# Adding rows and output biases in DRAM by an accumulating transfer instead of on GpSimd, and giving the root its constant as a bias

## The chip, the cores and the metric

The kernel runs on one core of one Trainium2 chip. The metric is device time in microseconds (us) of one execution, and lower is better. In this text PE is TensorE, PEld its weight loads, DVE is VectorE, ACT is ScalarE, POOL is GpSimd, and SP is SyncE, which here only issues transfers. "Sequence" means one of the four batch entries, counted from 0.

## The reference

The input x has 4 sequences of 2048 tokens with 512 features, all in fp32. With xn the layer norm of x, the output is x + attention(xn) + ffn(xn).

```python
xn = (x - mean) / sqrt(var + 1e-5)                  # over the 512 features
qkv = xn @ qkv_w.T + qkv_b                          # 16 heads of 32
attn = softmax(q @ k.T * 32 ** -0.5)
att = (attn @ v) @ proj_w.T + proj_b
idx = top_k(xn[:, 0, :] @ Wr + br, 2)               # two of 8 experts per sequence
ffn = sum over the two of (gelu(xn @ W1[e] + b1[e]) @ W2[e] + b2[e]) / 2
out = x + att + ffn
```

What the change is about are two small pieces of this. The first is the term that each output row starts from: x + proj_b + (b2[e0] + b2[e1]) / 2. The second is the square root in the layer norm.

## The kernel before, in words

The work of a sequence is cut into *units*. A unit takes 4 heads (a group), 512 queries (a chunk `qc`) and 128 keys (`kt`). There are 16 units to a chunk, 4 chunks to a group, 4 groups to a sequence, 1024 units in all, and 22 units of lead before unit 0. One loop over `U` writes out by hand, for each engine, what belongs to a unit: the scores `s` with their shift (L725, L733), a first pass for the maxima `m` that runs 22 units ahead (L715, reduced by DVE in L855), the exponentials `p` on ACT (L849), and the weighting by v (`acc`, L745). POOL adds up the exponentials of a chunk (`add_weights`): it starts with L762 at `kt` 1, goes on with L766, and at `kt` 15 it issues a transfer that accumulates the last `p` into `psum` (L764). There are four `p` buffers, so the exponentials of a unit need the buffer that was used four units earlier.

The class `Plan` puts all the rest into slots at every second unit: products for the next q and k, v projections, the two expert layers (`w1`, `w2`), the output projection (`proj`), and, for the next sequence, statistics, root, normalisation and the block sums (`ws`, `tx`) on POOL. It also gives each load a unit at which SP issues it; SP issues everything in one queue, in the order in which the loop reaches it. All PSUM tiles come from one pool of 8 banks, taken in turn.

The places that the change touches:

- `load`, tag `row` (L373): for the first of the two experts (`k` = 0) a row tile of 128 tokens is loaded from x, for the second one from `part_dram`, where the first left its partial sum. In `w2`, DVE adds half of the expert's product to it (L633).
- `row_ready`: four units after a `k` = 0 row has been loaded, POOL adds the sequence's `bias` tile to it (L881). The `bias` tile is made once per sequence by `load_bias` and `sum_bias` (L662 to L664).
- `root` (L431): DVE adds EPS to the variances (L433), ACT takes the root (L434), DVE the reciprocal (L435), POOL makes the shift (L436, L437). It is called once for the 4 first tokens, four times at the start for sequence 0, and once each for sequences 1 to 3, one unit into group 2 of the sequence before.
- The lead: the 16 tiles of v of sequence 0 are projected one per unit (`project_v`, L514). The tile has two buffers (`vrow`), and each is stored to `v_dram` by SP two units later (L515). Calls put into `later(u, ...)` are made at the end of unit `u`.

Of the kernel before, what the change touches and what calls it, by code (L numbers as in the profile page):

```python
# [9 lines left out]
F32 = mybir.dt.float32  # L10
BF16 = mybir.dt.bfloat16
U32 = mybir.dt.uint32
AF = mybir.ActivationFunctionType
ALU = mybir.AluOpType
# [3 lines left out]
P = 128  # L18
# [4 lines left out]
EPS = 1e-5  # L23
CH = 512
# [13 lines left out]
class Plan:  # L38
# [6 lines left out]
    def __init__(self, B, DC, NCH, NT, TPC):  # L45
# [13 lines left out]
        for G in range(1, B * DC):  # L59
            b, g = divmod(G, DC)  # L60
# [16 lines left out]
        for b in range(1, B):  # L77
# [8 lines left out]
            for n in range(NT):  # L86
                self.extra.setdefault(q1 + 2 * (16 + n) + 1, []).append(("stats", b, n))
                c, i = divmod(n, TPC)
# [80 lines left out]
        for s in slots:  # L169
            for it in self.items.get(s, []):  # L170
                if it[0] == "w2":
                    rows_at[it[1], it[3]] = s + 3
                assert it[0] != "proj" or s - 2 * WARN >= rows_at[it[1], it[2]], (s, it)
                for tag, key in self.needs(it):
                    self.uses.append((s, tag, key))
                if it[0] == "w2" and it[4] == 0:
                    self.first_load["row", (it[1], it[3], 1, it[5])] = s + 4
        for s in range(slots[0], self.units):
# [13 lines left out]
        for u in range(2, self.units + 1, 2):  # L192
            kt, G = (u - 2) % NT, (u - 2) // self.per_group
# [45 lines left out]
def block_kernel(  # L239
# [16 lines left out]
    nc = tc.nc  # L256
    B, N, D = x.shape
    E = Wr.shape[1]
    DC = D // P
    NT = N // P  # L260
    NCH = N // CH
    TPC = CH // P
# [3 lines left out]
    LEAD = plan.lead  # L266

    ctx.enter_context(tc.manual_schedule())
    const = ctx.enter_context(tc.tile_pool(name="const", bufs=1))
# [11 lines left out]
        return slice(j * HD, (j + 1) * HD)  # L281


    xn_dram, t_dram, v_dram, att_dram, part_dram, ws_dram = {}, {}, {}, {}, {}, {}
    for b in range(B):
        for k in range(TOP_K):
            ws_dram[b, k] = tc.dram_tile([P, DC, D], F32, name=f"ws_dram_{b}_{k}")
# [1 line left out]
    for b in range(B):  # L289
        for c in range(NCH):  # L290
            xn_dram[b, c] = tc.dram_tile([P, DC, CH], F32, name=f"xn_dram_{b}_{c}")
            v_dram[b, c] = tc.dram_tile([P, TPC, D], F32, name=f"v_dram_{b}_{c}")
            att_dram[b, c] = tc.dram_tile([P, DC, CH], F32, name=f"att_dram_{b}_{c}")
            t_dram[b, c] = tc.dram_tile([P, DC, CH], F32, name=f"t_dram_{b}_{c}")
            for i in range(TPC):
                part_dram[b, c, i] = tc.dram_tile([P, D], F32, name=f"part_dram_{b}_{c}_{i}")
# [6 lines left out]
    def expert(b, k):  # L303
        if (b, k) not in experts:
            experts[b, k] = nc.values_load(
                chosen[b : b + 1, k : k + 1], engines=[SP], min_val=0, max_val=E - 1,
                skip_runtime_bounds_check_because="max_index gives columns of E scores",
            )
        return experts[b, k]
# [3 lines left out]
    def load_xt(t, b, p, i):  # L313

        if i in (1, 2, 3):
            src, h = xn_dram[b, 2 * p + (i == 3)], int(i != 1)
        else:
            src, h = t_dram[b, 2 * p + (i in (7, 6))], int(i in (4, 6))
        nc.sync.dma_start(t, src[:, 2 * h : 2 * h + 2, :])

    def load_wt(t, kind, b, n, i):


        r, h = {1: (0, 0), 2: (0, 1), 4: (1, 1), 6: (0, 0), 3: (0, 1), 7: (1, 0), 5: (1, 1)}[i]
        if kind == "qk":
            if i in (1, 2, 4):
                src = qkv_wT.rearrange("(c p) n -> p c n", p=P)[:, :, (1 - r) * D : (2 - r) * D]
            else:
                src = wqk_dram[r]
            nc.sync.dma_start(t[:, :, 0, :], src[:, 2 * h : 2 * h + 2, ts(n, P)])  # L330
            return
        if i in (1, 2, 4):
            src = W1[ds(expert(b, n), 1)].rearrange("o (c p) f -> p (o c) f", p=P)
        else:
            src = ws_dram[b, n]
        for q in range(2):
            nc.sync.dma_start(t[:, :, q, :], src[:, 2 * h : 2 * h + 2, ts(2 * q + r, P)])

    def x_rows(b, c):
        return x[b, ts(c, CH), :].rearrange("(t p) d -> p t d", p=P)  # L340

    def load(tag, key):
        name = f"{tag}_" + "_".join(str(k) for k in (key if isinstance(key, tuple) else (key,)))
        shape = {"xq": [P, DC, CH], "xt": [P, 2, CH], "xl": [P, TPC, D], "wb": [P, DC, D],
                 "wt": [P, 2, 2, P], "row": [P, D], "prow": [P, D]}.get(tag, [P, TPC, P])
        t = stream.tile(shape, F32, tag=tag, name=name, bufs=BUFS[tag])
        held[tag, key] = t
        if tag == "xq" and key[0] == "stage":
            return t
        if tag == "xq":  # L350
            nc.sync.dma_start(t, xn_dram[key])
        elif tag == "xt":
            load_xt(t, *key)
        elif tag == "wt":
            load_wt(t, *key)
        elif tag == "v":
            b, g, c = key
            nc.sync.dma_start(t, v_dram[b, c][:, :, ts(g, P)])
        elif tag == "xl" and key[0] == "at":
            nc.sync.dma_start(t, att_dram[key[1:]])  # L360
        elif tag == "xl" and key[0] == "w1raw":
            src = W1[ds(expert(*key[1:]), 1)].rearrange("o (c p) f -> p (o c) f", p=P)
            nc.sync.dma_start(t, src)
        elif tag == "xl":
            nc.sync.dma_start(t, x_rows(*key[1:]))
        elif tag == "wb" and key[0] == "proj":
            nc.sync.dma_start(t, proj_wT.rearrange("(c p) n -> p c n", p=P))
        elif tag == "wb" and key[0] == "v":
            nc.sync.dma_start(t, qkv_wT.rearrange("(c p) n -> p c n", p=P)[:, :, 2 * D :])
        elif tag == "wb":  # L370
            src = W2[ds(expert(*key[1:]), 1)].rearrange("o (c p) f -> p (o c) f", p=P)
            nc.sync.dma_start(t, src)
        elif tag == "row":  # L373
            b, c, k, i = key
            src = part_dram[b, c, i] if k else x[b, c * CH + i * P : c * CH + (i + 1) * P, :]
            nc.sync.dma_start(t, src)
        else:
            nc.sync.dma_start(t, part_dram[key])
        return t
# [3 lines left out]
    make_identity(nc, ident)  # L383
    ident_b = const.tile([P, P], BF16, name="ident_b")
    nc.vector.tensor_copy(ident_b, ident)
    ones = const.tile([P, HD], F32, name="ones")
    nc.gpsimd.memset(ones, 1.0)
    ones_b = const.tile([P, P], BF16, name="ones_b")
# [4 lines left out]
    for i in range(2):  # L393
        t = const.tile([P, TPC, GH, HD], BF16, name=f"spread{i}")
# [17 lines left out]
    for n in range(2):  # L412
        wkq.append(stream.tile([P, DC, D], F32, tag="h", name=f"wkq_{n}", bufs=2))
        src = qkv_wT.rearrange("(c p) n -> p c n", p=P)[:, :, (1 - n) * D : (2 - n) * D]
# [5 lines left out]
    for n in range(2):  # L420
        src = qkv_wT.rearrange("(c p) n -> p c n", p=P)[:, :, (1 - n) * D : (2 - n) * D]
# [8 lines left out]

    def root(mv, sd, nb, a, z, np_=P):  # L431

        nc.vector.tensor_scalar(sd[:np_, a:z], mv[:np_, a:z, 1], EPS, None, ALU.add)  # L433
        nc.scalar.activation(sd[:np_, a:z], sd[:np_, a:z], AF.Sqrt)  # L434
        nc.vector.reciprocal(sd[:np_, a:z], sd[:np_, a:z])  # L435
        nc.gpsimd.tensor_tensor(nb[:np_, a:z], mv[:np_, a:z, 0], sd[:np_, a:z], ALU.mult)  # L436
        nc.gpsimd.tensor_scalar(nb[:np_, a:z], nb[:np_, a:z], -1.0, None, ALU.mult)  # L437
# [21 lines left out]
    mv, sd, nb = stat_tiles("first")  # L459
# [31 lines left out]
    hT, bias, b1s = {}, {}, {}  # L491
# [169 lines left out]
    def sum_bias(t, other, pb):  # L661
        nc.gpsimd.tensor_tensor(t, t, other, ALU.add)  # L662
        nc.gpsimd.tensor_scalar(t, t, 0.5, None, ALU.mult)
        nc.gpsimd.tensor_tensor(t, t, pb, ALU.add)  # L664


    mv, sd, nb = stat_tiles(0)

# [34 lines left out]
    def later(u, do):  # L703
        waiting.setdefault(u, []).append(do)
# [119 lines left out]
    for n in range(2):  # L824
        later(3 - LEAD, lambda n=n: nc.sync.dma_start(wqk_dram[n], wkq[n]))
    sum_bias(*load_bias(0))
    row_ready = {}

    for U in range(-LEAD, plan.units):
        second = U >= 0  # L830
        first_pass = U + LEAD if U + LEAD < plan.units else None
        chunk, kt = divmod(U, NT)
        b, g, qc, _ = place(U) if second else (0, 0, 0, 0)
# [42 lines left out]
        if before is not None and kt == (12 if keys == 4 else 14):  # L876
            divide(before)
            later(U + 3, lambda w=before: nc.sync.dma_start(
                att_dram[w[0], w[2]][:, w[1], :], att[w]))
        for t, key in row_ready.pop(U, []):  # L880
            nc.gpsimd.tensor_tensor(t, t, bias[key[0]], ALU.add)  # L881
        if second:
            add_weights(U)

# [10 lines left out]
        for step, sb, n in plan.extra.get(U, []):  # L895
# [10 lines left out]
            else:  # L906
                c, i = divmod(n, TPC)
# [10 lines left out]
        for do in waiting.pop(U, []):  # L918
            do()
        for s, tag, key in loads.get(U, []):  # L920
            t = load(tag, key)
            if tag == "row" and key[2] == 0:
                row_ready.setdefault(U + 4, []).append((t, key))
        if g == 2 and qc == 0 and kt == 0 and second and b + 1 < B:
            new_bias = load_bias(b + 1)
        if g == 2 and qc == 0 and kt == 5 and second and b + 1 < B:
            sum_bias(*new_bias)

        for n, c in ((16, NCH - 1), (1, NCH - 2)):
            if U == plan.units - n:  # L930
                tags = ("xq", "xq") if c == NCH - 1 else ("xl", "h")
                t, rows = (
                    stream.tile([P, TPC, D], F32, tag=tag, name=f"end_{c}_{n}",
                                bufs=BUFS.get(tag, 2))
                    for n, tag in enumerate(tags)
                )
# [7 lines left out]
    U = plan.units  # L944
# [72 lines left out]
```

## Time and profile before

| | |
|---|---|
| time before, median of 3 runs | 5038.61 us (5038.29 to 5046.06) |
| profiled execution, its own time | 5042.55 us |
| profiled execution, its span | 5040.8 us |
| mean granted TensorE clock | 0.997 |
| busy, share of the span | PE 98%, DVE 74%, ACT 47%, POOL 88% |
| POOL, row plus bias (L881) | 64 instructions, 83.8 us |
| POOL, accumulating transfer (L764) | 63 issues, 54.6 us |
| DVE, variance plus EPS (L433) | 8 instructions |

The profile comes from one execution, whose own time stands in the table. Busy shares are averages over the whole span. A busy PE is not PE at its peak. Where the granted clock falls below 1, PE is busy and slow.

### The profile page before, as it was taken

The numbers are of one execution on the slowest core, as the hardware profiler recorded it, in microseconds if no ns is written. First come the engines' busy times: TensorE is split into PE (matmuls) and PEld (weight loads), VectorE is DVE, ScalarE is ACT, GpSimd is POOL, SyncE is SP. The second block draws the span as 40 slices with busy tenths as digits, with TensorE's granted clock in tenths as the row PEclk, the third lists the DMA queues.
The fourth block names the chain that finished last, engine by engine and source line by source line (L and its number), as shares of the span: only waits on it lengthen the run. The fifth ranks groups of instructions, "written<-read, shape, count | busy, mean of one in ns | idle before, by whom it ended". The sixth has DMA issues, their size and how long they took to land. (4 is left out here: it accounts for less than half of the span.)

```text
span 5040.8 us, 107883 instructions
## 1 busy us (share of the span) xinstructions
PE 4947.0 (98%) x45028; PEld 1725.8 (34%) x45028; DVE 3740.2 (74%) x5909; ACT 2394.0 (47%) x4406; POOL 4429.2 (88%) x1498
## 2 busy tenths in 40 slices
PE   8999999999999999999999999999999999999998
PEld 2333333333333333333333333333333333333332
DVE  5777887777777788777777777877777777777762
ACT  1445445454444545454444444555444445454453
POOL 2799998999898998999889998999988988999981
PEclk9999999999999999999999999999999999999999
DMA  6333334433233434434224234434423343323312
GB/s 219 111 103 117 115 96 127 142 122 109 80 107 104 126 107 122 140 114 141 89 86 125 85 121 118 146 122 136 134 70 106 100 123 101 101 80 101 107 62 95
DMA packets 297128, 568.16 MB, mean 113 GB/s; under 512 B 24636, under 2 KB 144188, under 8 KB 279744
## 3 DMA queue, kind: packets, MB, share of 16 engines
q1 hardware_dynamic: 287568, 495.19, 29.4%
q0 software_dynamic: 9072, 66.06, 6.7%
q8 instruction: 354, 5.80, 0.5%
q14 instruction: 134, 1.10, 0.1%
HBM read 367.44 MB, written 127.66 MB: 98 GB/s over the span
## 5 line engine op out<-in xcount | busy, mean ns | idle before, releaser
L766 POOL TENSOR_TENSOR psum<-psum,p 128x2048 f32<-128x2048 f32 x819 | 3722.4, 4545 | 167.6 <-ACT p L849 129.2
L849 ACT ACTIVATE p<-s 128x512 f32<-128x512 f32 x4096 | 2118.0, 603 | 2364.9 <-PE m L715 2181.8
L855 DVE TENSOR_REDUCE mx<-m 128x1 f32<-128x512 f32 x4096 | 2544.2, 684 | 570.1 <-PE m L715 569.8
L733 PE MATMUL s<-qT,kT 32*128 32x512 f32 x8192 | 1919.1, 588 | 0.0
L715 PE MATMUL m<-kT,qT 32*128 32x512 f32 x8192 | 1911.3, 590 | 6.4 <-ACT h L524 3.4
L715 PEld LDWEIGHTS m<-kT,qT 32*128 32x128 f32 x8192 | 920.9, 184 | 334.9 <-issue 244.7
L745 PE MATMUL acc<-p,v 128*32 128x512 f32 x8192 | 988.5, 600 | 37.0 <-ACT p L849 37.0
L733 PEld LDWEIGHTS s<-qT,kT 32*128 32x128 f32 x8192 | 768.6, 185 | 29.2 <-issue 7.3
L485 PE MATMUL ops<-wb_w,h 128*32 128x512 f32 x4096 | 466.0, 595 | 0.6 <-ACT p L849 0.2
L745 PEld LDWEIGHTS acc<-p,v 128*32 128x32 f32 x8192 | 214.2, 109 | 737.0 <-ACT p L849 420.5
L762 POOL TENSOR_TENSOR psum<-p,p 128x2048 f32<-128x2048 f32 x63 | 287.5, 4563 | 203.2 <-ACT p L849 203.2
L754 DVE TENSOR_TENSOR sacc<-acc,sacc 128x512 f32<-128x512 f32 x448 | 309.9, 692 | 158.3 <-PE acc L745 158.3
L485 PE MATMUL hps<-xt,wt_w 128*32 128x512 f32 x3584 | 411.0, 596 | 2.5 <-ACT p L849 2.0
L725 PE MATMUL s<-negm,ones_b 32*128 32x512 bf16 x4096 | 405.7, 385 | 6.2 <-ACT p L849 5.9
L485 PE MATMUL qkps<-xt,wt_qk 128*32 128x512 f32 x3360 | 387.8, 599 | 9.8 <-ACT p L849 9.2
L725 PEld LDWEIGHTS <-ones_b 32*128 32x128 bf16 x4096 | 103.2, 91 | 858.2 <-issue 858.1
L870 DVE RECIPROCAL sums<-sums 128x128 f32<-128x128 f32 x252 | 237.6, 943 | 0.7 <-ACT sums L784 0.7
L485 PEld LDWEIGHTS ops<-wb_w,h 128*32 128x32 f32 x4096 | 120.0, 109 | 308.6 <-issue 229.8
L633 DVE SCALAR_TENSOR_TENSOR row<-ops,row 128x512 f32<-128x512 f32 x128 | 88.4, 691 | 170.3 <-PE ops L485 116.3
L485 PE MATMUL prps<-wb_proj,xl_at 128*32 128x512 f32 x1792 | 203.9, 595 | 0.3
L485 PEld LDWEIGHTS hps<-xt,wt_w 128*32 128x32 f32 x3584 | 103.3, 109 | 268.2 <-issue 186.1
L485 PEld LDWEIGHTS qkps<-xt,wt_qk 128*32 128x32 f32 x3360 | 97.3, 110 | 273.9 <-issue 181.6
(123 smaller groups left out, 1981.6 us busy)
## 6 DMA issues: line engine op xcount, KB each, us to landing
xt<-t_dram SPq DMA_DIRECT2D x181, 512.0 KB, 4.3
xt<-xn_dram SPq DMA_DIRECT2D x133, 512.0 KB, 5.0
psum<-p POOLq DMA_DIRECT2D x63, 1024.0 KB, 8.2
part_dram<-row SPq DMA_DIRECT2D x128, 256.0 KB, 2.0
v_dram<-v SPq DMA_DIRECT2D x64, 256.0 KB, 2.7
wt_w<-ws_dram SPq DMA_DIRECT2D x128, 128.0 KB, 3.3
v<-v_dram SPq DMA_DIRECT2D x64, 256.0 KB, 4.9
row<-in_x_dram SPq DMA_DIRECT2D x64, 256.0 KB, 6.5
```

Source lines behind the costliest of these rows:

```text
L485: nc.tensor.matmul(pp[rows_of(j), :], lhsT[:, rows_of(j)], rhs, start=(first and n == 0), stop=(last and n == len(terms) - 1),)
L633: nc.vector.scalar_tensor_tensor(row, pp, 0.5, row, ALU.mult, ALU.add)
L715: nc.tensor.matmul(t, qT[b, g, qc][r, ts(i, P)], kT[b, g, kc][r, :], start=True, stop=True)
L725: nc.tensor.matmul(tiles[j], ones_b[r, :], negm[b, g, qc][r, :], start=True, stop=False)
L733: nc.tensor.matmul(tiles[j], kT[b, g, kt // TPC][r, ts(kt % TPC, P)], qT[b, g, qc][r, :], start=False, stop=True,)
L745: nc.tensor.matmul(acc[r, :], held["v", (b, g, kt // TPC)][:, (kt + n) % TPC, r], pT[u + n][:, j, :], start=(n == 0), stop=(n == 1),)
L754: nc.vector.tensor_tensor(t, acc, t, ALU.add)
L762: nc.gpsimd.tensor_tensor(psums[b, g, qc], pT[u - 1], pT[u], ALU.add)
L766: nc.gpsimd.tensor_tensor(psums[b, g, qc], psums[b, g, qc], pT[u], ALU.add)
L849: nc.scalar.activation(pT[U][:, j, :], tiles[j], AF.Exp, scale=SCALE)
L855: nc.vector.tensor_reduce(dst, t, AX.X, ALU.max, negate=True)
L870: nc.vector.reciprocal(sums[before][:, q], sums[before][:, q])
```

## The change

There is a new DRAM tensor per chunk, `base_dram`. SP copies the chunk's rows of x into it from DRAM to DRAM (`copy_rows`, 1 MB in 512 rows of 2 KB). Later POOL issues a transfer that accumulates the `bias` tile, repeated four times, into it (`add_bias`, also 512 rows of 2 KB). A `k` = 0 row is then loaded from `base_dram` and is complete when it lands, so L881 and `row_ready` go.

For sequence 0 the four copies are made at unit -18 and the four additions at unit -10. For sequence b + 1 the copies are made at units 6, 8, 10 and 12 of group 2 of sequence b, and the four additions together at unit 16, the first of that group's second chunk. The instructions of PE stand in the same order as before, and SP's other transfers too.

In `root`, DVE's addition of EPS goes; ACT takes EPS as the bias operand of the root and reads the variances itself.

```diff
@@ Plan
+                if it[0] == "w2" and it[4] == 0 and it[1]:
+                    self.first_load["row", (it[1], it[3], 0, it[5])] = (
+                        (it[1] - 1) * self.per_seq + 2 * self.per_group + NT + 1
+                    )
...
+            base_dram[b, c] = tc.dram_tile([P, TPC, D], F32, name=f"base_dram_{b}_{c}")
...
-            src = part_dram[b, c, i] if k else x[b, c * CH + i * P : c * CH + (i + 1) * P, :]
+            src = part_dram[b, c, i] if k else base_dram[b, c][:, i, :]
...
+    eps = const.tile([P, 1], F32, name="eps")
+    nc.gpsimd.memset(eps, EPS)
...
     def root(mv, sd, nb, a, z, np_=P):
-        nc.vector.tensor_scalar(sd[:np_, a:z], mv[:np_, a:z, 1], EPS, None, ALU.add)
-        nc.scalar.activation(sd[:np_, a:z], sd[:np_, a:z], AF.Sqrt)
+        nc.scalar.activation(sd[:np_, a:z], mv[:np_, a:z, 1], AF.Sqrt, bias=eps[:np_])
         nc.vector.reciprocal(sd[:np_, a:z], sd[:np_, a:z])
...
+    def copy_rows(b, c):
+        nc.sync.dma_start(base_dram[b, c], x_rows(b, c))
+
+    def add_bias(b, c):
+        nc.gpsimd.dma_start(
+            base_dram[b, c], bias[b].unsqueeze(1).to_broadcast([P, TPC, D]), accum_op=ALU.add
+        )
...
     sum_bias(*load_bias(0))
-    row_ready = {}
+    for c in range(NCH):
+        later(4 - LEAD, lambda c=c: copy_rows(0, c))
+        later(12 - LEAD, lambda c=c: add_bias(0, c))
...
-        for t, key in row_ready.pop(U, []):
-            nc.gpsimd.tensor_tensor(t, t, bias[key[0]], ALU.add)
...
-            t = load(tag, key)
-            if tag == "row" and key[2] == 0:
-                row_ready.setdefault(U + 4, []).append((t, key))
+            load(tag, key)
...
             sum_bias(*new_bias)
+            for c in range(NCH):
+                later(U + 1 + 2 * c, lambda c=c: copy_rows(b + 1, c))
+        if g == 2 and qc == 1 and kt == 0 and second and b + 1 < B:
+            for c in range(NCH):
+                add_bias(b + 1, c)
```

More of the change, by code (lines that the diff above doesn't have):

```diff
@@ L281, in rows_of @@
         return slice(j * HD, (j + 1) * HD)
-    xn_dram, t_dram, v_dram, att_dram, part_dram, ws_dram = {}, {}, {}, {}, {}, {}
+    base_dram, xn_dram, t_dram, v_dram, att_dram, part_dram, ws_dram = {}, {}, {}, {}, {}, {}, {}
     for b in range(B):
```

## The prediction

> **What bounds the kernel now.** I read the page's busy rows first, then the waits, then the timeline around every place where PE stands still.
>
> ```profile
> PE 4947.0 (98%) x45028; PEld 1725.8 (34%) x45028; DVE 3740.2 (74%) x5909; ACT 2394.0 (47%) x4406; POOL 4429.2 (88%) x1498
> ```
>
> PE is the bound: 94 us of the 5040.8 are free of it, about 17 of them before the lead and 6 in the last products. PE's order stays, so the change is worth only what it takes from or adds to those 94 us, and to the stretches in which PE runs at a lower granted clock. POOL at 88% isn't the bound, and its 83.8 us of row additions are no gain as such. The waits say where POOL and DVE reach PE:
>
> ```profile
> ACT p L849 <- DMA psum<-p: 36.3, 9, 7.4
> ...
> ACT sd L434 <- DVE sd L433: 30.8, 7, 6.5
> ```
>
> (total us, times, longest.) The second is the root. Its timeline in sequence 0, columns start, duration, engine:
>
> ```profile
> 761.40 1.28 ACT L434 ACT_TABLE_LOAD   x1
> 761.74 4.90 DVE L433 TENSOR_SCALAR sd<-mv 128x16 f32<-128x16 f32 x1
> 761.82 4.78 POOL L762 TENSOR_TENSOR psum<-p,p 128x2048 f32<-128x2048 f32 x1
> ...
> 766.67 0.21 ACT L434 ACTIVATE sd<-sd 128x16 f32<-128x16 f32 x1 [3.99 <-DVE sd L433]
> ...
> 767.43 1.21 PE L715 MATMUL m<-kT,qT 32*128 32x512 f32 x1 [3.45 <-ACT h L524]
> ```
>
> The same DVE instruction takes 170 ns at the median of its eight. Here it ends with POOL's pass; in the other two big roots too (4.29 us and 4.28 us). ACT waits behind it, and PE for ACT. Then comes a second price, PE's clock (the last columns are granted clock, DMA share, GB/s):
>
> ```profile
> 767.40:774.00 6.60, 6.57 (x30) 1.77 (x34) 2.89 (x5) 3.34 (x5) 3.50 (x3) 0.53 0.66 185
> ...
> 3207.00:3211.00 4.00, 4.00 (x28) 1.20 (x24) 1.54 (x3) 1.00 (x3) 2.92 (x1) 0.57 0.91 240
> ```
>
> The first wait is POOL's lateness at chunk ends: the accumulating transfer L764 goes out late, and ACT gets its `p` buffer late.
>
> ```profile
> 1160.23 1.07 PE L485 MATMUL qkps<-xt,wt_qk 128*32 128x512 f32 x8 [0.97 <-ACT p L849]
> 2068.41 1.09 ACT L849 ACTIVATE p<-s 128x512 f32<-128x512 f32 x2 [3.25 <-DMA psum<-p]
> 3446.61 0.66 PE L455 MATMUL xt<-ident,xl_normal 128*128 128x128 f32 x4 [2.07 <-ACT p L849]
> 4791.84 1.50 PE L485 MATMUL hps<-xt,wt_w 128*32 128x512 f32 x12 [0.75 <-ACT p L849]
> ```
>
> **What it removes.** *The root.* In sequence 0 ACT would take the root at 762.7, right after its table load, since the variances are there from 753.1. What is left is two table loads and the root, 1.28 + 0.21 + 1.28 = 2.8 us of ACT; a gelu with its tables takes 4.5 us of ACT and costs PE 1.16 us, so this costs PE nothing much. DVE then waits at the reciprocal for ACT until 763.2, some 1.4 us, with the maxima queued behind it. The reciprocal is not held by POOL: L870 never takes more than 953 ns of a 943 ns mean under a POOL that is 88% busy. Gain: 3.45 us plus 6.6 us x (1 - 0.53) = 3.1, 6.5 us. In the third big root (3200) 1.46 plus 4 us x (1 - 0.57) = 1.7, 3.2 us. In the second (1979.7) ACT is in a gelu and a table load until 1983.8 anyway, and the reciprocal holds DVE as long as L433 did: nothing of its 1.48. At the start five small L433 (0.14 to 0.17 us) leave the chain to the first product: 0.3 us.
>
> *64 row additions*, 1.28 us each. They matter in the chunks before a wait: 3 lie before the 0.97, 6 (7.7 us of POOL) before 2068, where PE stood 1.29 us, 6 before the 2.07, and 3 before the 0.75. ACT's waits there are 2.9 to 4.0 us or less, below what is freed, so all four go: 5.1 us. The larger ones (4.73 us at 2368, 2.47 at 3049, 4.97 at 4939) have no row addition in their chunk and stay. DVE's waits for L881 (9.8 us) end no wait of PE.
>
> Together 15 us; I count 14, as the root keeps something.
>
> **What it adds.** *Four copies in the lead, 4 MB on SP's queue.* They stand behind the store of v tile 1 and ahead of that of tile 2.
>
> ```profile
> 68.03 0.81 SPq L825 DMA_DIRECT2D wqk_dram<-wkq  x2
> 68.93 4.28 SPq L515 DMA_DIRECT2D v_dram<-v  x2
> ...
> 77.48 0.32 SPq L581 DMA_DIRECT2D ws_dram<-xl_w1raw  x1
> ```
>
> ```profile
> 77.40 0.69 DVE L514 TENSOR_TENSOR v<-vps,bv_bc 128x512 f32<-128x512 f32 x1 [1.73 <-DMA v_dram<-v]
> ...
> 81.46 0.69 DVE L514 TENSOR_TENSOR v<-vps,bv_bc 128x512 f32<-128x512 f32 x1 [0.97 <-PE vps L485]
> ```
>
> The reader is to see that tile 3 (77.40) waited for tile 1's store, which took 8.4 us for 256 KB as two 1 MB stores were ahead of it. In the same way tile 4 (81.46) will wait for tile 2's store, and so for four copies. Their price is not in the trace. The nearest row, the 1 MB `wqk` stores, landed 2.95 us apart (71.93 and 74.88). The Trainium skill speaks against it: "DMA: Bandwidth & Descriptors", section "Latency and other measured facts", gives copies between HBM tensors 207 to 214 GB/s, which makes an estimate of 4.9 us per MB. Tile 1's data is through at about 75.3. Tile 2 lands 2.4 us after the copies: at 89.5 by the row, at 97.3 by the rule. PE doesn't stand at once: a unit takes 4.64 us and 5 of 8 banks, so with tile 4's bank held it can still do a unit and two maxima, to about 86.9. It goes on 0.8 us after the landing. PE's stop is 3.4 us by the row, 11.2 by the rule, and a stop of 3.45 us has cost 3.1 us of clock. I take 4.2 us per MB, between, nearer the rule since the row moves data on one HBM side only: 8.4 + 3.1 = 11.5 us (ends 3.4 and 14.3). Behind SP's blocked queue stand the store of `ws_dram`, the next `xl_w1raw` load and POOL's block sums, some 10 to 15 us late; the products that need them come 30 us later.
>
> *Four additions in the lead.* POOL idles from 102 to 131.85, so their issue is free. But SP's transfers keep the engines 0.92 busy from 110 to 128, and v stores must land within two units; one already held DVE 1.7 us at 128.4. An accumulated MB lands after 8.2 us (`psum<-p`), so four are up to 33 us of shared engines. Bounds 0 and 10 us; I take 2.5, because DVE's delay has to pass the same 5 us of banks.
>
> *Copies in the loop*, 12 of them, two units (10 us) apart, each under 5 us. The tightest load behind one is the second normalisation load of each sequence: it landed at 822.2 for 829.4, at 2034.2 for 2038.8. The copy ahead is through before SP reaches it. Zero; without that cover about 1 to 5 us each.
>
> *Additions in the loop*, four together on POOL, three times, at the start of a chunk, where POOL waits anyway:
>
> ```profile
> 839.04 0.90 POOL L764 DMA_DIRECT2D psum<-p  x1 [0.30 <-POOL psum L766]
> 847.62 4.56 POOL L762 TENSOR_TENSOR psum<-p,p 128x2048 f32<-128x2048 f32 x1 [7.69 <-ACT p L849]
> ```
>
> L764 takes 0.87 us with 128 rows of 8 KB; an addition has 512 rows of 2 KB. In proportion that is 3.5 us; by the skill (the same page, "Anatomy of one DMA — SWDGE (gpsimd) path") generating descriptors is small and many go out before it shows, so 0.9. Four make 3.5 to 14 us. I take 2 us each, 8: it fits the 7.69 above, at 2061 it takes the place of six row additions, and at 3277 POOL has 4.89 + 1.71 us of idle time. I count 1 us for all, with 22 us of transfer beside loads that have 8.9 us to spare or more.
>
> **Sum:** -14 + 11.5 + 2.5 + 1 = +1 us, on the profiled execution's 5042.55 (span 5040.8 and 1.75 around it). That execution is 3.9 us above the median of 5038.61, so the forecast is 5040 us. About 0.2%, 10 us, is what a measurement of this kernel can tell from no change.
>
> **Rivals.**
> - *Faster.* Copies run at the row's 2.95 us or better, and PE's stop stays below 3.4 us and keeps the clock: -14 + 2 to 4 = 5028. For it: both directions of transfer show about 3 us per MB alone. Against: a copy loads HBM twice. Chance 0.22.
> - *Slower, by POOL.* An addition costs by its rows, 3.5 us. Then 14 us in the chunk meet 11.6 us of idle time at 840 to 865 (7.69 + 2.97 + 0.90), none at 2061, where POOL is 6.5 us late instead of on time, and 10 us at 3277. The lateness shows at the next chunk end as ACT's wait for `psum<-p`: 2.4 + 5.7 + 4 us for PE and up to 3 us of clock each, 12 to 21 us: 5052 to 5061. It decides from about 2.5 us an issue. For it: 512 rows instead of 128. Against: the rule. Chance 0.18.
> - *Slower, in the lead.* Copies of 6 us per MB (PE stops 15.6 us, 18.7 with the clock) and 6 us for the additions: -14 + 25, 5050. Chance 0.14.
> - *That rows from DRAM come too late:* the first is loaded at 153.9, when the additions have long been issued, and used 32 us later. I give it no chance of its own.
>
> **Numbers.** Same 0.46, faster 0.22, slower 0.18 + 0.14 = 0.32. The likeliest case alone spans 5030 to 5048. For 8 in 10 the range goes from 5026, the faster case with all gains, to 5061, POOL's case.
>
> **What would show it.** The root's ACT wait of 3.99 gone and PE without a gap near 764. One DVE wait of 7 to 16 us for `v_dram<-v` near 81, a gap of PE after 87, and a low clock behind it. Copies landing 4 to 5 us apart. The four waits at chunk ends gone, those at 2368, 3049 and 4939 still there. The POOL issue of an addition near 2 us. I am wrong if tile 2's store lands before 86, or if POOL is later than before at the ends of the chunks with additions.

## The result, and the profile after

The changed kernel takes 5057.18 us in the median of 7 runs (5053.79 to 5058.61), against 5039.66 us for the kernel before (7 runs, 5036.28 to 5047.1). The ratio is 1.0029, with a 95% interval of 1.0018 to 1.004: slower by some 15 us (17.5 by the medians). The profiled execution took 5054.43 us, span 5052.7. A profile line has the line numbers of its own kernel: in the changed kernel L514 of the kernel shown has become L520, L715 L730, L764 L779 and L849 L866; the copy is L673 and the addition L677. In the experiments they lie a few lines off.

Busy times, from the page of the changed kernel:

```profile
PE 4952.9 (98%) x45028; PEld 1730.8 (34%) x45028; DVE 3726.8 (74%) x5901; ACT 2395.2 (47%) x4406; POOL 4372.0 (87%) x1451
```

POOL lost 57 us of work (4429.2 to 4372.0) and the kernel got slower: POOL's busy time was not what PE waited for. The waits (total us, times, longest) say what took its place:

```profile
DVE v L520 <- DMA v_dram<-v: 28.3, 4, 13.1
ACT p L866 <- DMA psum<-p: 28.2, 6, 7.9
```

The second was 36.3, 9, 7.4: three of the waits at chunk ends are gone. The first is new at this size. Both of its large parts lie in the lead. SP's queue, then DVE and PE in the timeline (start, duration):

```profile
67.55 6.59 SPq L673 DMA_DIRECT2D base_dram<-in_x_dram  x4
74.24 3.55 SPq L521 DMA_DIRECT2D v_dram<-v  x1
```

```profile
88.53 0.69 DVE L520 TENSOR_TENSOR v<-vps,bv_bc 128x512 f32<-128x512 f32 x1 [8.49 <-DMA v_dram<-v]
...
141.92 0.69 DVE L520 TENSOR_TENSOR v<-vps,bv_bc 128x512 f32<-128x512 f32 x1 [13.12 <-DMA v_dram<-v]
```

```profile
89.28 2.67 PE L730 MATMUL m<-kT,qT 32*128 32x512 f32 x4 [4.47 <-DVE v L520]
```

```profile
142.67 2.67 PE L730 MATMUL m<-kT,qT 32*128 32x512 f32 x4 [7.10 <-DVE v L520]
...
153.17 3.09 PE L730 MATMUL m<-kT,qT 32*128 32x512 f32 x9 [0.73 <-DVE v L520]
```

The four copies stand ahead of the store of a v tile; DVE waits 8.49 us for that buffer and PE 4.47 us for DVE. Later the four additions do the same to other v stores, and PE stands 7.10 and 0.73 us. SP's queue shows how:

```profile
122.39 1.17 SPq L521 DMA_DIRECT2D v_dram<-v  x1
123.61 1.03 SPq L324 DMA_DIRECT2D xt<-xn_dram  x1
133.43 0.80 SPq L324 DMA_DIRECT2D xt<-t_dram  x2
...
139.84 13.62 SPq L521 DMA_DIRECT2D v_dram<-v  x3
```

The store issued at 122.39 lands at 141.80, 19.4 us later, and DVE goes on. The next tile is ready at 126.0, but its store is issued only at 139.84: ahead of it in the queue, SP waits 8.7 us, until 133.42, for the store of `t_dram` that the `xt` load reads. With each stop the clock goes low (the columns are the stretch, its length, busy time and instructions of PE, PEld, DVE, ACT and POOL, granted clock, DMA share, GB/s):

```profile
84.80:96.00 11.20, 6.73 (x30) 2.06 (x32) 6.15 (x10) 0.00 (x0) 0.00 (x0) 0.70 0.75 255
...
140.00:150.40 10.40, 7.73 (x32) 2.23 (x36) 3.08 (x5) 0.00 (x0) 0.00 (x0) 0.51 1.08 319
150.40:161.00 10.60, 9.87 (x48) 2.76 (x40) 8.54 (x15) 0.00 (x0) 4.80 (x7) 0.84 0.33 114
```

The best single number is when unit 0 begins its exponentials: 156.5 us before, 24.3 us later after (26.6 later than in e2 below, which has none of these eight transfers). From there to the last unit the changed kernel wins back 12.4 us, so that it is 11.9 us late at the end. Between units 128 and 160 (the root of sequence 1) it wins 5.7 us, between units 640 and 704 (the third big root and the chunk end at 3444) 4.2 us.

### The profile page after: what moved, and what is told of

The parts are those of the page before. It is cut to its first block, busy times and chain, and to the rows that moved or that the text cites. A ratio compares the mean times of both kernels' runs of the same rounds, so it can differ in the third digit from the quotient of the medians.

```text
span 5052.7 us, 107823 instructions
## 1 busy us (share of the span) xinstructions
PE 4952.9 (98%) x45028; PEld 1730.8 (34%) x45028; DVE 3726.8 (74%) x5901; ACT 2395.2 (47%) x4406; POOL 4372.0 (87%) x1451
## 5 line engine op out<-in xcount | busy, mean ns | idle before, releaser
L866 ACT ACTIVATE p<-s 128x512 f32<-128x512 f32 x4096 | 2118.5, 602 | 2357.8 <-PE m L730 2162.5
L730 PE MATMUL m<-kT,qT 32*128 32x512 f32 x8192 | 1916.4, 590 | 13.7 <-DVE v L520 12.3
L730 PEld LDWEIGHTS m<-kT,qT 32*128 32x128 f32 x8192 | 925.4, 184 | 342.3 <-issue 244.8
```

The costliest lines, as they stand in the source:

```text
L730: nc.tensor.matmul(t, qT[b, g, qc][r, ts(i, P)], kT[b, g, kc][r, :], start=True, stop=True)
L866: nc.scalar.activation(pT[U][:, j, :], tiles[j], AF.Exp, scale=SCALE)
```

## The experiments

Each kernel ran beside the kernel before on the same chip. The ratios of their runs to it are compared; each has an interval of about 0.0008 to 0.0013 either way, 4 to 7 us. "Unit 0" is the start of its first exponentials in the profiled execution. In some executions, before among them, the full clock came at 22.7 us and in others, after among them, at 17 us; that alone is 2.3 us in the "unit 0" column and was not the change's.

| kernel | median us | ratio (95%) | unit 0 |
|---|---|---|---|
| before | 5039.66 to 5041.75 | 1 | 156.5 |
| after | 5057.18 | 1.0029 (1.0018 to 1.0040) | 180.8 |
| e1: root alone | 5039.05 | 0.9994 (0.9986 to 1.0002) | 156.4 |
| e2: sequence 0's rows by GpSimd | 5033.23 | 0.9982 (0.9975 to 0.9989) | 154.2 |
| e3: no additions in the lead | 5039.52 | 0.9997 (0.9988 to 1.0005) | 163.2 |
| e4: old root | 5063.31 | 1.0044 (1.0031 to 1.0058) | 183.1 |
| e5: three v buffers | 5051.58 | 1.0021 (1.0012 to 1.0029) | 175.0 |
| e6: only sequence 0 in DRAM | 5060.95 | 1.0042 (1.0028 to 1.0055) | 182.7 |
| e7: sequence 0 after the lead | 5029.42 | 0.9975 (0.9967 to 0.9984) | 154.1 |
| e8: plain writes in the lead | 5046.01 | 1.0010 (1.0004 to 1.0017) | 170.4 |
| e9: half of sequence 0, after the lead | 5031.01 | 0.9979 (0.9972 to 0.9987) | 154.1 |
| e10: sequence 0 spread | 5032.01 | 0.9982 (0.9974 to 0.9990) | 156.9 |
| e11: e9 with the old root | 5037.35 | 0.9993 (0.9985 to 1.0001) | 153.9 |

The theory at the start: the loss lies in the lead alone, copies and additions both, by way of the v stores; the root and the row additions gain about what was forecast. The rivals: the transfers in the loop cost something too; the copies alone cost; the gaps at the roots closed by a shift and not by the edit.

**e1, the root alone.**

```diff
-        nc.vector.tensor_scalar(sd[:np_, a:z], mv[:np_, a:z, 1], EPS, None, ALU.add)
-        nc.scalar.activation(sd[:np_, a:z], sd[:np_, a:z], AF.Sqrt)
+        nc.scalar.activation(sd[:np_, a:z], mv[:np_, a:z, 1], AF.Sqrt, bias=eps[:np_])
```

> The kernel before with the root's constant as a bias and nothing else of the change. If the losses of the change all lie in its row transfers and the root gives what its two gaps say (3.45 us and 1.46 us of PE, with the slow clock behind each), this is 9 to 10 us faster than before: about 5030 us, ratio 0.998. PE has no gap near 764 and no low clock at 767 to 774. If the rival holds, that those gaps closed in the changed kernel only because the lead had shifted what ran beside them, nothing is gained: 5039 us, ratio 1.000.

Measured: 0.9994, some 3 us, with an interval that just holds no change: between theory and rival. In its profile the root of sequence 1 gains 4.4 us (units 128 to 160) and the third 2.8 us (units 640 to 672), and neither has a low clock behind it, as the theory has it; but that execution, at 5035.2 us, is 4 us below e1's median. The size was left to e4 and e11.

**e2, sequence 0's rows by GpSimd.** No copy and no addition for sequence 0; POOL adds the bias to its 16 row tiles as before.

```diff
-    for c in range(NCH):
-        later(4 - LEAD, lambda c=c: copy_rows(0, c))
-        later(12 - LEAD, lambda c=c: add_bias(0, c))
+    row_ready = {}
...
+            if not k and b == 0:
+                src = x[b, c * CH + i * P : c * CH + (i + 1) * P, :]
...
```

> The changed kernel, but sequence 0 takes its rows from x and GpSimd adds the bias, as before; sequences 1 to 3 keep their copies and additions in DRAM. If the loss lies in the lead alone, 24 us of it go: about 5027 to 5031 us, some 10 to 13 us faster than before (ratio 0.9975), PE without the gaps at 84.8, 135.6 and 152.4. If the rival holds, that the twelve copies and additions in the loop cost about as much as the lead's four, it stays slower than before: 5045 us or more.

Measured: 0.9982, 9 us faster than before and 24 us faster than the changed kernel (1.0029 - 0.9982 = 0.0047). The whole loss was in the lead's eight transfers, and the rival, a cost of the loop's transfers, is out. The three gaps are gone.

**e3, no additions in the lead.** As the changed kernel, without the line `later(12 - LEAD, ...)`.

> The changed kernel without the four additions in the lead; the bias is left out of sequence 0's rows. If the additions are the larger part of the loss (gaps of 7.1 us and 0.7 us, and some 7 us of slow clock), about 15 us go: 5042 us, ratio 1.0005, with the gap at 84.8 (4.5 us) still there and those at 135.6 and 152.4 gone. If the rival holds, that the copies are the cost and the additions only fall into a stretch that was late already, it stays at 5053 to 5057 us.

Measured: 0.9997; 0.0032 or 16 us of the loss go with the additions, and 0.0015 or 8 us are left to the copies (e3 less e2). PE's first gap stays, and the others are gone. Here are the only gap of PE behind DVE in e3's lead, and the longest of DVE's waits:

```profile
88.84 2.66 PE L730 MATMUL m<-kT,qT 32*128 32x512 f32 x4 [4.04 <-DVE v L520]
```

```profile
88.10 0.69 DVE L520 TENSOR_TENSOR v<-vps,bv_bc 128x512 f32<-128x512 f32 x1 [8.11 <-DMA v_dram<-v]
```

**e5, three buffers for the v tiles.**

```diff
-        t = pair.tile([P, D], F32, tag="vrow", name=f"v_{b}_{n}")
+        t = pair.tile([P, D], F32, tag="vrow", name=f"v_{b}_{n}", bufs=3)
...
```

> The changed kernel with three buffers for the v tiles instead of two; every transfer is as in the changed kernel. If the loss reaches PE only through these buffers (VectorE waits for a store, PE for VectorE), one more unit of 4.6 us is covered: the gap of 4.5 us at 84.8 goes with its slow clock, the 7.1 us at 135.6 fall to some 2.5 us: 5038 to 5046 us. If the rival holds, that the transfers simply lack bandwidth and PE runs into another late transfer, the gaps move to other places with the same sum: 5054 us or more.

Measured: 1.0021, 4 us better than the changed kernel instead of 11 to 19, and 4 us is within the two intervals. The copies' gap is gone, but the additions' gap has grown:

```profile
150.07 2.07 PE L730 MATMUL m<-kT,qT 32*128 32x512 f32 x2 [16.14 <-DVE v L520]
```

PE arrived earlier and then stood until 150.07, when the additions were nearly through (the last landed at 150.98); in the changed kernel PE's second stop after the additions ended at 153.17. So the buffers only carry the wait. The rival was the better reading: in this stretch transfers lack time on the DMA engines, and PE goes on when the backlog is through.

**e8, plain writes in the lead.** The four transfers of sequence 0 as before in place, queue and size, without `accum_op`.

```diff
-            base_dram[b, c], bias[b].unsqueeze(1).to_broadcast([P, TPC, D]), accum_op=ALU.add
+        if b == 0:
+            nc.gpsimd.dma_start(base_dram[b, c], src)
+        else:
+            nc.gpsimd.dma_start(base_dram[b, c], src, accum_op=ALU.add)
```

> The changed kernel with the four transfers of sequence 0's bias in the lead as plain writes (same queue, same 1 MB each, same shapes) in place of accumulating ones; x is so left out of sequence 0's rows. If it is the accumulation that makes them slow (9 us per MB against about 3 us for a plain MB), they are through some 20 us sooner, the gaps at 135.6 and 152.4 go, and 10 to 16 us of the loss with them: 5041 to 5047 us, ratio 1.000 to 1.001. If the rival holds, that 2048 rows of 2 KB on GpSimd's queue or the 4 MB as such take the time, it stays at 5055 to 5058 us.

Measured: 1.0010, 11 us better than the changed kernel by the medians (5057.2 to 5046.0) and 10 by the ratios, at the near end of what the theory asked. Beside the copies' gap, one of 0.73 us is left at 141.5, and as plain writes they still cost 6.5 us against none (e3, 5039.5). The transfers landed at 117.7, 120.7, 125.7 and 133.0; accumulating, at 122.5, 133.6, 140.2 and 149.3. The DMA queues between 110 and 155 us say why: packets, MB, share of 16 engines, first of the changed kernel, then of e8 (q0 has POOL's transfers, q1 SP's).

```profile
q0 software_dynamic: 2112, 4.19, 52.7%
q1 hardware_dynamic: 3351, 6.54, 41.3%
```

```profile
q1 hardware_dynamic: 4146, 7.14, 44.6%
q0 software_dynamic: 1088, 4.19, 25.2%
```

For the same 4.19 MB the accumulating transfers make twice the packets and hold the engines twice as long: 0.527 x 45 / 4 = 5.9 us of all 16 engines per MB, against 2.8 us. With them the two queues hold the engines for 94% of the stretch, in e8 for 70%.

**e4, the old root, and e6, only sequence 0 in DRAM.** e4 is the changed kernel with e1's edit taken back. e6 is the changed kernel without this, and with GpSimd adding the rows of sequences 1 to 3:

```diff
-            for c in range(NCH):
-                later(U + 1 + 2 * c, lambda c=c: copy_rows(b + 1, c))
-        if g == 2 and qc == 1 and kt == 0 and second and b + 1 < B:
-            for c in range(NCH):
-                add_bias(b + 1, c)
```

> The changed kernel with the root of before: rows and biases in DRAM alone. If the parts simply add, the root is worth what it was alone (ratio 0.9994, about 3 us; 7 us in the profiled execution) and this is 3 to 7 us slower than the changed kernel: 5060 to 5064 us, ratio 1.0035 to 1.0045, with PE's gap behind ACT's wait for DVE at sequence 1's root back. If the rival holds, that the later work in the lead has moved the root off its wait by itself, it equals the changed kernel: 5057 us, ratio 1.003.

> The changed kernel, but only sequence 0's rows go through DRAM (the four copies and four additions of the lead); the rows of sequences 1 to 3 come from x and GpSimd adds their bias, as before. If the loop's part of the change is a gain of about 5 us (the stalls at the ends of chunks near 2064, 3438 and 4791 gone), this is 4 to 6 us slower than the changed kernel: 5061 to 5063 us, ratio 1.004. If the rival holds, that the twelve copies and additions in the loop cost something as well, it is as fast as the changed kernel or faster: 5050 to 5057 us.

Measured: e4 1.0044, e6 1.0042, both slower than the changed kernel by 0.0015 and 0.0013, 8 and 7 us by ratios and 6 and 4 us by medians, with intervals that are as wide. Both go the theory's way, but neither is clear of its interval. The page's waits show e6's part apart from the root; these rows are of e1 (GpSimd adds all rows), e6 and e2 (the loop's rows in DRAM):

```profile
ACT p L850 <- DMA psum<-p: 42.5, 11, 7.7
```

```profile
ACT p L869 <- DMA psum<-p: 35.1, 9, 7.2
```

```profile
ACT p L866 <- DMA psum<-p: 28.4, 6, 7.8
```

Only where the loop's rows are in DRAM are the waits at chunk ends fewer. That POOL's issues don't eat this up is to be seen in the changed kernel at the start of two such chunks:

```profile
858.92 5.18 POOL L677 DMA_DIRECT2D base_dram<-bias  x4
866.45 4.56 POOL L777 TENSOR_TENSOR psum<-p,p 128x2048 f32<-128x2048 f32 x1 [2.35 <-ACT p L866]
```

```profile
3291.41 5.17 POOL L677 DMA_DIRECT2D base_dram<-bias  x4
3296.70 4.54 POOL L777 TENSOR_TENSOR psum<-p,p 128x2048 f32<-128x2048 f32 x1
```

Four issues take 5.2 us together, 1.3 us each; at 866 POOL still waits for ACT behind them.

**e7, sequence 0 after the lead.** Chunks 0, 3 and 2 are copied in units 2, 4 and 6 and get their bias in unit 16; chunk 1 is on GpSimd.

```diff
+    for n, c in enumerate((0, 3, 2)):
+        later(2 + 2 * n, lambda c=c: copy_rows(0, c))
+    for c in (0, 3, 2):
+        later(NT, lambda c=c: add_bias(0, c))
...
```

> The changed kernel with sequence 0's copies and additions put off: chunks 0, 3 and 2 are copied in units 2, 4 and 6 and get their bias in unit 16, when the v stores are done and the transfers idle; chunk 1, whose rows are used first, comes from x with GpSimd's additions. If the loss is where the transfers stand and not that they are made, it is as fast as with no such transfer for sequence 0 (5033 us) or 1 us faster: 5031 to 5034 us, ratio 0.998. If the rival holds, that a megabyte accumulated in DRAM costs PE some 4 us wherever it stands, 12 us come back: 5045 us.

Measured: 0.9975, the rival (12 us for three additions wherever they stand) is out: here they landed at 247.9, 256.6 and 262.9, as slow as in the lead, with no gap of PE beside them (from 239 to 263 PE is busy throughout at full clock, while the engines' share is 1.04). Two of chunk 0's row tiles are loaded at 201.7 and 212.4, before the additions are issued at 233.7, so this kernel leaves out two biases; e9 mends that.

**e9, chunks 1 and 0 on GpSimd, 3 and 2 in DRAM after the lead; e11, the same with the old root; e10, all in DRAM but spread.**

```diff
+    for n, c in enumerate((3, 2)):                                   # e9, e11
+        later(2 + 2 * n, lambda c=c: copy_rows(0, c))
+        later(NT, lambda c=c: add_bias(0, c))
...
+    for c, at, then in ((1, 4 - LEAD, 12 - LEAD), (0, -6, 0), (3, 2, NT), (2, 4, 2 * NT)):   # e10
+        later(at, lambda c=c: copy_rows(0, c))
+        later(then, lambda c=c: add_bias(0, c))
...
```

> The changed kernel with sequence 0 split: the rows of chunks 1 and 0, used early, come from x with GpSimd's additions; those of chunks 3 and 2, first loaded in unit 103, are copied in DRAM in units 2 and 4 and get their bias in unit 16. In e7_after_lead two of chunk 0's four row tiles were loaded before their bias was added, so two biases were left out; here nothing is. If e7's time came from the place of the transfers, this is as fast: 5028 to 5032 us, ratio 0.9975 to 0.998. If the rival holds, that it came from the two additions that were left out or from chance, it is at 5033 us or above, as with all of sequence 0's rows on GpSimd.

> The changed kernel with all rows in DRAM, but sequence 0's transfers spread: chunk 1 is copied and gets its bias where the changed kernel does it, chunk 0 is copied 6 units before the end of the lead and gets its bias in unit 0, chunks 3 and 2 are copied in units 2 and 4 and get theirs in units 16 and 32. If it is the queue of four megabytes at once that holds the v stores back, one copy (2.65 us) is hidden and one addition (some 9 us) makes VectorE wait by 4 us at most, so PE stands 0 to 3 us: 5027 to 5034 us, ratio 0.997 to 0.999. If the rival holds, that any accumulating megabyte in the lead stops PE for about 4 us and brings the slow clock, it is at 5036 to 5042 us.

> As e9_later_rows, but with the root of before; against e9 on the same chip it prices the root. If the root is worth what the gaps say (3.45 us and 1.46 us of PE with the slow clock), it is 8 to 10 us slower than e9: 5037 to 5040 us. If it is worth what the kernel with the root alone showed in its median (ratio 0.9994, 3 us), it is 3 us slower than e9.

Measured: e9 0.9979, e10 0.9982. Both beat the kernel before by 9 to 11 us and the changed kernel by 24 to 25; between e2, e7, e9 and e10 these runs don't decide. In e10 the transfers left in the lead (chunk 1's copy and addition, then chunk 0's copy) cost PE 2.8 us; these runs don't tell which of them. DVE gets to one v tile at 130.15 instead of 125.81 (e9). No wait of PE's is shown; it is inside a stretched group, first e9, then e10:

```profile
130.03 2.00 PE L732 MATMUL m<-kT,qT 32*128 32x512 f32 x16
```

```profile
130.00 5.26 PE L730 MATMUL m<-kT,qT 32*128 32x512 f32 x16
```

e11 prices the root: 0.0014 or 6 to 7 us more than e9, between the two numbers expected. In its profile the root of sequence 1 is as it was before: DVE's addition held, PE's gap, and the low clock behind it. At the third root, PE has its gap, but the clock stays full:

```profile
759.22 4.26 DVE L442 TENSOR_SCALAR sd<-mv 128x16 f32<-128x16 f32 x1
...
764.26 1.62 PE L733 MATMUL m<-kT,qT 32*128 32x512 f32 x2 [2.80 <-ACT h L533]
```

```profile
764.40:771.60 7.20, 6.91 (x30) 1.76 (x34) 2.73 (x5) 3.17 (x5) 4.19 (x2) 0.53 0.76 254
3200.00:3204.00 4.00, 4.00 (x41) 1.46 (x44) 2.73 (x6) 2.23 (x5) 2.52 (x1) 1.00 0.80 252
```

## Why the prediction was right and wrong

The range (5026 to 5061) held the time, but by luck: its upper end came from the rival by POOL, which did not happen. The likeliest case, no change at 5040, did not happen either. What did is the rival "slower, in the lead", to which I gave 0.14 and which I put at 5050. Its sum of +25 us for the lead is what e2 measured (24), but with its terms the other way round: 18.7 for the copies and 6 for the additions, where 8 and 16 were measured. So its sum was luck too. The gains came to 9 to 11 us (e2, e9, e10), not 14.

- *The copies: mechanism right, size a little high.* Taken at 4.2 us per MB, 11.5 us in all. They landed at 79.8, 82.8, 85.0 and 87.8, 2.65 us apart: the row of the `wqk` stores (2.95) was right. The rule of the Trainium skill ("DMA: Bandwidth & Descriptors", "Latency and other measured facts", 4.9 by my estimate) is given for tiles of 16 KB rows; it differs from what was measured here, where 1 MB in 2.65 us is 396 GB/s, and I had chosen a value nearer the rule. PE's stop was 4.5 us and the clock was low for 6.8 us behind it (predicted 8.4 + 3.1); e3 less e2 gives 8 us in the runs and 9 in the profiles. By the row alone, 3.4 + 3.1, it would have been 6.5.
- *The additions in the lead: the step that failed.* "Bounds 0 and 10 us; I take 2.5, because DVE's delay has to pass the same 5 us of banks." Measured: 16 us (e3), above the upper bound. The duration was right: four took 37.5 us to land, where 33 were expected. What I didn't do is to add up engine time. Both terms were to be had from before: the queue of its 63 `psum<-p` transfers in the page, and a window over the stretch.

```profile
q0 software_dynamic: 9072, 66.06, 6.7%
```

```profile
110.00:155.00 45.00, 45.00 (x391) 12.83 (x390) 35.58 (x58) 1.19 (x2) 10.54 (x9) 1.00 0.67 230
```

An accumulating MB costs 0.067 x 5040.8 / 63 = 5.4 us of all 16 engines. The engines were 0.67 busy, so 45 x 0.33 = 14.9 us were free, and four additions ask for 21.4: 6.5 us over, which some transfer has to be late by. (The stretch is chosen with the result known: it is where the additions ran.) SP's v stores share the engines with them, and the banks had cover for less than that. The sum is not the whole, however. e8's plain writes ask for 4 x 2.8 = 11.3 us, less than is free, and still cost 6.5 us. It matters where the free time lies:

```profile
110.00:128.00 18.00, 18.00 (x160) 4.95 (x160) 12.01 (x19) 0.00 (x0) 0.00 (x0) 1.00 0.92 321
128.00:155.00 27.00, 27.00 (x235) 7.88 (x234) 23.56 (x39) 1.19 (x2) 10.54 (x9) 1.00 0.51 169
```

Only 18 x 0.08 = 1.4 us of it came before 128, and the additions were issued at 112; what is late then also holds SP's queue, as shown above. PE's stops were 7.8 us. The clock was at half speed for 10.2 and 3.4 us; PE worked in 11.0 us of that, which is 5.5 us of work. The other 4 of the 17.6 us by which unit 0 is later than in e3 are in no wait that the views show.
- *The root: mechanism right, size too large.* Predicted 6.5 + 3.2 + 0.3, 10 us. The gap of 3.45 became 0.79, the third 1.16, and the second stayed (1.41), as said. The profiles show 5.7 and 2.8 us for the changed kernel's two roots; the runs 3 (e1), 6 to 7 (e11) and 6 to 8 (e4). One reason is shown: the low clock at the third root, 1.7 of the 10 us, stood in the trace of before and not in those of e4 and e11, which have the same root. Without it the profiles' 8.5 us are 6.8, which is what e11 and e4 measured; e1's interval holds it. At the second root it is the other way round: full clock in before, and 3.4 us at half clock in e2, e3, e4, e6, e10 and e11. The price of a clock dip read from one execution is not a price of every execution.
- *The row additions: mechanism right for at least two of the four waits, size not shown closely.* Predicted 5.1 us. The four waits of PE at chunk ends (0.97, 1.29, 2.07 and 0.75) are gone, and those at 2368, 3049 and 4939 are still there (5.92, 1.58 and 4.53). But in e1, where GpSimd adds all rows, only the first three stay (0.95, 1.01 and 1.70), so the fourth, 0.75, was not theirs; in e6, where GpSimd adds those of sequences 1 to 3, only the first and the third (1.73 and 1.99). e2 less e1 is 6 us, e6 less the changed kernel 4 to 7, with intervals of 5 and 9 us either way.
- *Copies and additions in the loop: right.* 0 and 1 us; nothing is seen that must be theirs. PE's gaps at the ends of the three chunks with additions are 0.55, none over 0.5 and 1.42 us (before: none over 0.5 at the first two, and 0.71), but without them e6 has 0.53 at the first and e1 1.12 at the third. An issue took 1.3 us, nearer the 0.9 (the time of L764, taken on the word of the Trainium skill, "DMA: Bandwidth & Descriptors", "Anatomy of one DMA — SWDGE (gpsimd) path") than the 3.5 by rows, so the rival by POOL, which decided from 2.5 us an issue, is out.
- *The signs.* DVE's wait of 7 to 16 us (8.49), the gap of PE with the low clock behind it and the vanished wait at the root were where they should be; copies 4 to 5 us apart were wrong, and for the additions in the lead I had named no sign at all.

## What to carry to other kernels

When a transfer is added, add up DMA engine time for the stretch in which it will run: the queue's share of the span in the page, over its transfers, is the price of one, and the DMA share of that stretch says what is free; look also at whether it is free when the transfer starts, and at what stands behind it in the queue. A sum that fits is not enough (e8). Taking work from a busy engine that PE doesn't wait for gains only the few waits that it ends; here 57 us of POOL were worth about 6. Issued after the lead, the same transfers cost nothing that these runs show (e9 against e2), so their place is to be tried before the mechanism is given up: e9, the changed kernel with sequence 0's early rows left on GpSimd, beats both kernels at 5031 us.

## What the hardware showed that I had not expected

- An accumulating transfer into DRAM made twice the packets of a plain one (2112 against 1088 for 4.19 MB) and held the 16 engines for 5.9 us per MB against 2.8.
- They landed 6.6 to 11.1 us apart per MB in the lead, and 8.7 and 6.3 us apart after it in e7, where the engines were no less busy (share 1.04 from 239 to 263). An estimate from the 5.9 us of engine time: much closer they can't follow each other.
- A copy from DRAM to DRAM in rows of 2 KB took 2.65 us per MB, no more than a store from SBUF (2.95).
- The gap of PE at the third root, 1.46 us, had the low clock behind it in before, and not in e4 (1.45) or e11 (1.46). The one at the second root (1.40 to 1.49) had none in before, e1 and e9, and 3.4 us of it in e2, e4 and e11.
- The group row of the additions gives 2292 ns as the mean of one issue, but 20.6 us as the busy time of all 16: the records overlap, and 1.3 us each is what POOL loses.
